# Row transposes two blocks ahead, a Newton inverse deviation, sorting by single operations and paired output projections in a convolution, attention and mixture-of-experts kernel

## The chip, the cores and the metric

The kernel runs on one core of a Trainium2 chip. The metric is the device time of one execution in microseconds, the median of several runs. The kernel before took 1325.14 us (three runs, 1323.45 to 1325.67). A core has five engines that run their own instruction lists in order and meet at semaphores: PE (TensorE, matrix products), ACT (ScalarE), DVE (VectorE), POOL (GpSimd) and SP (which only starts transfers here). PEld is PE's loading of the stationary operand.

## The reference

The input is two images of 256 channels and 56 x 56 pixels. Layer 0 is a grouped linear attention without softmax, folded with a normalisation, then a sum with its input and a ReLU. Layer 1 treats the 3136 pixels of each image as tokens of 256 numbers:

```
t = t + attn(ln(t))          # 4 heads of 64, causal softmax, then W_proj
x = ln(t)
probs = softmax(x @ gate_w + gate_b)          # 8 experts
top2_vals, top2_idx = top_k(probs, 2)
t = t + sum over the two experts e of  prob_e * (gelu(x @ W1[e] + b1[e]) @ W2[e] + b2[e])
```

`ln` subtracts the mean and divides by the square root of the variance plus 1e-5. All of it is computed in 32-bit floats.

## The kernel before

Layer 0 comes first, up to about 90 us. Then comes attention for image b=0 and for b=1, up to about 885 us, and then the experts, up to the end. From attention on, the order of every engine's instructions is the order in which the program writes them: nothing is moved by a scheduler.

**Attention** (`attend`). The queries of an image are cut in 7 blocks `i` of 448, and the heads in two pairs `hp`. One group is one (i, hp): it walks over tiles of 128 keys, one tile a step. In step n, in this order: `between` (other work, below), the tasks that have come due, `values` of the step three back (L689, the products of the exponentials with v), then `scores` of step n (L649 on PE, L657 exponentials on ACT, L659 mask on DVE, L671 or L667 the running sum of the exponentials, `acc`, on DVE). Where the step three back is the first of its group, `values` comes after `scores`. After the last `values` of a group the result is copied out of its one PSUM tile (L699 on ACT, then L700 on DVE adds the other half), and the next group's first `values` may only write that tile after L700. `values` then puts `sum_rows` on the list `later`, with the step at which it is due: it sums `acc` over the partitions on PE (L716, tile `sp`), and a chain of transfers through DRAM, `invert`, more transfers and `scale` (L748) brings the inverse back. The list is sorted when a task has run, and the head of the list is the only one looked at.

**Work beside attention.** `between` alternates: in one step it draws two pieces from `queue` (`pull(2)`), in the next it runs pieces of the projections to q, k and v (L535, L554, with transposes L514). A piece is what a generator does up to its next `yield True`. `tokens(b)` is the generator of the token work: `project_out` (L598, the output projection, tile by tile of 128 tokens, with DVE additions and statistics), then `dispatch`, which forms the gate, ranks the tokens by expert and scatters their rows to DRAM (L1217). For b=0 it runs beside b=1's attention; for b=1 it runs beside the experts, where each block draws two pieces, or three while rows are scattered.

In `dispatch`, `inverse_deviation` (L162) takes one ACT square root and one DVE reciprocal for all tokens. Then follow the softmax of the gate (L955 to L967, its exponential on ACT at L963), two rounds of choosing the best expert (L979 to L986), `both` (L991), the two PE products that rank the tokens (L1001, L1003), and some twenty small DVE operations that give every token its slot (to L1081). `small_piece` stands between groups of them: three yields for b=0, one for b=1.

**Experts** (`experts`). 105 blocks of 128 rows. Iteration n writes: the fetch of a group of three blocks (up to n+6), `load` (L1280 to L1289, DVE, up to n+2), `hidden(n)` (L1335 on PE, L1344 gelu on ACT), `inputs(n+1)` (transposes L1312 on PE, tile `tp`; the copy `xT`, L1316, on ACT), `weights` for the blocks ahead (L1323, DVE), `outputs(n-3)` (L1354 on PE, L1364 on DVE, then stores and scatters), and pieces. `hidden(n)` needs `xT` of block n and the weights copied for it. The tile pool of `xT` has three buffers, that of `tp` two.

Of the kernel before, what the change touches and what calls it, by code (L numbers as in the profile page):

```python
# [27 lines left out]
def conv_attn_moe_kernel(  # L28
# [410 lines left out]
    def layer1(nm, general):  # L439

        with ExitStack() as whole:
# [147 lines left out]
            def project_out(b, qT, done):  # L589

                for first, m, k in pairs():
                    while done() < (first + m - 1) * P + k:
                        yield False
                    for n in range(first, first + m):
                        o = n * P
                        ps = bank(f"pp_{b}_{n}")
                        for c in range(NH):
                            nc.tensor.matmul(  # L598
                                ps[:k, : C + E], qT[:, c, o : o + k], wpr[:, c, :],
                                start=(c == 0), stop=(c == NH - 1),  # L600
                            )
                        t = ts[b][:k, n, : C + E]
                        nc.vector.tensor_tensor(t, t, ps[:k, : C + E], ALU.add)
                        stats(b, n, 1, k, bg, f"o{nm}{b}")
                        if b == 0:
                            nc.sync.dma_start(out=rest_d[:k, n], in_=t[:, :C])
                        yield True

                    for _ in range(2 if b == 0 else 0):
                        yield True  # L610

            def attend(
# [63 lines left out]
                def values(n):  # L676
# [19 lines left out]
                    if last:  # L696

                        yh = qT[:, hp, i * W : (i + 1) * W]
                        nc.scalar.copy(yh, yp[:, 0, :W])  # L699
                        nc.vector.tensor_tensor(yh, yh, yp[:, 1, :W], ALU.add)  # L700
                        del yps[hp, i]
                        later.append((clock[0], sum_rows, hp, i, yh))

                def queue_of(hp, i):

# [229 lines left out]
            def dispatch(b):  # L935

                t = ts[b]
                tail = chunk(NCH - 1)
                inverse_deviation(b, 0, NCH)
                yield True  # L940

                def small_piece():

                    for _ in range(1 if b else 3):
                        yield True

                def small(name, last=E, dt=F32):
                    return g1.tile([P, NCH, last], dt, tag=name, name=f"{name}_{nm}{b}")

                def wide(ap):  # L950
                    return ap.to_broadcast([P, NCH, E])

                pr = small("lg")
                red = small("red", 1)
                nc.vector.tensor_tensor(  # L955
                    pr, t[:, :, C : C + E], wide(t[:, :, RSTD : RSTD + 1]), ALU.mult
                )
                nc.vector.tensor_tensor(
                    pr, pr, gb.unsqueeze(1).to_broadcast([P, NCH, E]), ALU.add
                )  # L960
                nc.vector.tensor_reduce(red, pr, AX.X, ALU.max)
                nc.vector.tensor_tensor(pr, pr, wide(red), ALU.subtract)
                nc.scalar.activation(pr, pr, AF.Exp)  # L963
                yield from small_piece()
                nc.vector.tensor_reduce(red, pr, AX.X, ALU.add)
                nc.vector.reciprocal(red, red)
                nc.vector.tensor_tensor(pr, pr, wide(red), ALU.mult)  # L967
                yield from small_piece()


# [5 lines left out]
                for k in range(2):  # L976
                    top = wts[b][:, :, k : k + 1]
                    one = small(f"one{k}")
                    nc.vector.tensor_reduce(top, src, AX.X, ALU.max)  # L979
                    nc.vector.tensor_tensor(at, src, wide(top), ALU.is_equal)  # L980
                    nc.vector.tensor_tensor(at, at, ids, ALU.mult)
                    yield from small_piece()
                    nc.vector.tensor_reduce(red, at, AX.X, ALU.max)
                    nc.vector.tensor_tensor(one, at, wide(red), ALU.is_equal)
                    if k == 0:
                        nc.vector.scalar_tensor_tensor(left, one, -2.0, pr, ALU.mult, ALU.add)  # L986
                        src = left
                    picks.append(one)
                    yield from small_piece()
# [7 lines left out]
                if b:  # L997
# [7 lines left out]
                nc.vector.tensor_tensor(  # L1005
                    ranks, rank[:, : NCH * E].rearrange("p (t e) -> p t e", e=E), both, ALU.subtract
                )
                tot = g1.tile([P, E, NCH], F32, tag="tot", name=f"tot_{nm}{b}")
                nc.vector.tensor_copy(tot, total[:, : NCH * E].rearrange("p (t e) -> p e t", e=E))
                yield from small_piece()  # L1010
                def few(name, dt=F32):
                    return g1.tile([P, E], dt, tag=name, name=f"{name}_{nm}{b}")
# [6 lines left out]
                else:  # L1019
# [11 lines left out]
                    ends.rearrange("p e t -> p (e t)"), ones_t,  # L1031
                    tot.rearrange("p e t -> p (e t)"), 0.0, ALU.mult, ALU.add,
                )

                first = few("first")
                nc.vector.tensor_tensor(first, ends[:, :, NCH - 1], cnt, ALU.subtract)
                nc.vector.tensor_tensor(ends, ends, tot, ALU.subtract)
                slot = g1.tile([P, NCH, E], F32, tag="both", name=f"slot_{nm}{b}")
                nc.vector.tensor_tensor(slot, ranks, ends.rearrange("p e t -> p t e"), ALU.add)
                yield from small_piece()  # L1040

                low = few("low")
# [22 lines left out]
                    return few.unsqueeze(1).to_broadcast([P, NCH, E])  # L1065

                nc.vector.tensor_tensor(part, slot, spread(lim), ALU.is_lt)
                nc.vector.tensor_tensor(part, part, spread(low), ALU.mult)
                yield from small_piece()
                nc.vector.tensor_tensor(slot, slot, spread(base), ALU.add)  # L1070
                nc.vector.tensor_tensor(slot, slot, part, ALU.add)
                yield from small_piece()
                for k in range(2):
                    nc.vector.tensor_tensor(at, slot, picks[k], ALU.mult)
                    nc.vector.tensor_reduce(red, at, AX.X, ALU.add)
                    flat = red.rearrange("p t o -> p (t o)")
                    nc.vector.tensor_scalar(
                        idxs[b][:, k, :], flat, -float(known[b][0] * P), None, ALU.add
                    )
                    if b and k == 0:  # L1080
                        nc.vector.tensor_scalar(t[:, :, SLOT], flat, 1.0, None, ALU.add)  # L1081
                    yield from small_piece()

                def one_hot(eb, w):

                    nc.vector.tensor_copy(eblks[b], eb[:, :w])
                    hot = g1.tile([E, w], F32, tag="hot", name=f"hot_{nm}{b}")
                    nc.vector.tensor_tensor(hot, eb[:E, :w], row.to_broadcast([E, w]), ALU.is_equal)
                    yield from small_piece()
                    for _ in range(1 if b else 3):  # L1090
                        yield True
                    bp = bank(f"bp_{b}", (P, KH, w))
                    for k in range(KH):
                        nc.tensor.matmul(bp[:, k, :], b1s[:, k, :], hot, start=True, stop=True)
                    nc.vector.tensor_copy(b1bs[b], bp)
                    ranked[b] = True
                    yield from small_piece()

                def first_blocks():
# [5 lines left out]
                        upto.unsqueeze(1).to_broadcast([P, MIXED, E]),  # L1105
                        ALU.is_ge,
                    )
                    eb = g1.tile([P, MIXED], F32, tag="eb", name=f"eb_{nm}{b}")
                    nc.vector.tensor_reduce(eb, past, AX.X, ALU.add)
                    yield from small_piece()  # L1110
                    step = g1.tile([P, MIXED], F32, tag="step", name=f"step_{nm}{b}")
                    nc.vector.tensor_scalar(step, number[:, :MIXED], nfull, -float(E), ALU.is_ge, ALU.mult)
                    nc.vector.tensor_tensor(eb, eb, step, ALU.add)
                    nc.vector.tensor_scalar(step, number[:, :MIXED], nfull, 0.0, ALU.subtract, ALU.max)
                    nc.vector.tensor_tensor(early, eb, step, ALU.add)
                    yield from one_hot(early, FULL0)
# [116 lines left out]
            def experts(w1s, w2s, b2s, ex, es, ps6, between, need, written):  # L1233
# [156 lines left out]
                for n in range(-1, NBLK + LATE):  # L1390
                    while len(fetched) * GB <= min(n + 6, NBLK - 1):
                        fetched.append(fetch(len(fetched)))
                    while len(groups) * GB <= min(n + 2, NBLK - 1):
                        groups.append(load(len(groups), *fetched[len(groups)]))
                    if n < 0:
                        ids.extend(experts_of(0))
                    if 0 <= n < NBLK:
                        act[n] = hidden(n, xin.pop(n), wb.pop(n))
                    if n + 1 < NBLK:
                        xin[n + 1] = inputs(n + 1, groups[(n + 1) // GB])  # L1400
                    for m in (n + 1, n + 2):
                        if m < NBLK and m not in wb:
                            wb[m] = weights(m)
# [416 lines left out]
```

## Time and profile before

| what | value |
|---|---|
| time | 1325.14 us, median of 3 |
| span of the profiled execution | 1323.5 us, granted PE clock 0.993 on the mean |
| PE idle in 60:130 us | 1.20 + 0.56 us |
| PE idle at 131, 199 and 517 us, before L689, until L700 | 1.49, 1.02 and 1.49 us |
| first expert block (L1335) | 886.58 us |
| last expert block ends | 1297.2 us |
| last row scatter of b=1 (L1217) | 1020.87 us |
| first fetch of rows of b=1 by blocks (L1256) | 1034.43 us |

The profile says for each group of instructions how long it was busy and what ended the idle time before it. A line of the timeline has: start in us, length in us, engine, source line, operation, written tile <- read tiles, the tile's size in the array, the shape, the number of instructions merged, and, in brackets, idle time before it and what ended it. The starts of matrix products are recorded; their ends are modelled, so the spacing of starts says more than the lengths.

### The profile page before, as it was taken

The page shows a single profiled execution, that of the slowest core. Times are in us where ns is not written, and L with a number is a line of the kernel's source. Part 1 is how long each engine was busy: PE and PEld are TensorE (multiplying, and loading weights), DVE is VectorE, ACT ScalarE, POOL GpSimd, SP SyncE. Part 2 cuts the span into 40 slices and gives each one's busy share as a digit, 9 for nine tenths or more (in the row PEclk, how much of TensorE's full clock was granted, in tenths as well). Part 3 has the DMA queues.
Part 4 walks back from the last instruction along what each step waited for, and adds up shares of the span by engine and source line. Part 5 has one row for each costly group of instructions (what it writes and reads, how often), then busy time and mean ns, then how long its engine had stood idle before and what let it go on. Part 6 is the DMA issues. An engine that isn't in the chain of part 4 may idle for free.

```text
span 1323.5 us, 28216 instructions
## 1 busy us (share of the span) xinstructions
PE 1281.4 (97%) x10647; PEld 811.4 (61%) x10647; DVE 791.9 (60%) x1657; ACT 613.2 (46%) x1247; POOL 311.8 (24%) x300
## 2 busy tenths in 40 slices
PE   8999999999999999989999999998999999999994
PEld 7875444444444444434444444447999999999994
DVE  1582555757777654565958788765754344555552
ACT  0145554555555555455554456554333333344441
POOL 1113110000000111110004444000176012765541
PEclk9999999999999999999999999999999999999997
DMA  9993000000000000100001112441254333666642
GB/s 298 384 327 131 16 24 25 24 16 24 9 17 13 21 1 8 41 9 9 16 17 56 53 54 87 176 139 40 81 169 156 93 112 100 187 208 198 187 153 71
DMA packets 111048, 123.96 MB, mean 94 GB/s; under 512 B 20095, under 2 KB 100620, under 8 KB 110904
## 3 DMA queue, kind: packets, MB, share of 16 engines
q1 hardware_dynamic: 96664, 92.89, 22.8%
q0 software_dynamic: 10416, 26.00, 5.9%
q10 hardware_dynamic: 3824, 3.18, 0.8%
q8 instruction: 88, 1.44, 0.5%
q14 instruction: 56, 0.46, 0.1%
HBM read 63.04 MB, written 60.81 MB: 94 GB/s over the span
## 4 chain that ended last, share of the span: by engine, by line
PE 92%; DVE 2%; ACT 2%; DMA 1%; issue 1%; POOL 1%; SPq 0%; DVEq 0%; ACTq 0%; POOLq 0%
PE yp_f L689 21%; PE sc_f L649 19%; PE ht_f L1335 14%; PE yp_f L1354 13%; PE qk_f L535 6%; PE pp_f L598 4%; PE v_f L554 4%; PE cp L321 3%; PE gram L252 3%; PE tp_f L1312 2%; ACT st_f L657 1%; PE sp_f L716 1%; PE yo_f L1477 1%; DVE acc_f L671 1%; PE xp_f L514 1%
## 5 line engine op out<-in xcount | busy, mean ns | idle before, releaser
L657 ACT ACTIVATE st_f<-sc_f 128x896 f32<-128x896 f32 (+5 forms) x400 | 333.8, 838 | 293.8 <-PE sc_f L649 265.4
L671 DVE TENSOR_TENSOR acc_f<-acc_f,st_f 128x896 f32<-128x896 f32 (+5 forms) x372 | 366.5, 985 | 170.0 <-ACT st_f L657 163.1
L689 PE MATMUL yp_f<-st_f,v_f 64*64 64x448 f32 (+6 forms) x3184 | 342.0, 505 | 7.7 <-DVE qT_f L700 6.5
L649 PE MATMUL sc_f<-qT_f,kT_f 64*64 64x448 f32 (+6 forms) x3184 | 342.3, 501 | 0.0
L1344 ACT ACTIVATE g_f<-ht_f,b1b 128x128 f32<-128x128 f32 x420 | 120.1, 369 | 223.5 <-PE ht_f L1335 223.4
L1335 PE MATMUL ht_f<-xT_f,w_f 128*128 128x128 f32 x1680 | 205.8, 276 | 5.8 <-ACT xT_f L1316 5.8
L649 PEld LDWEIGHTS sc_f<-qT_f,kT_f 64*64 64x64 f32 x3184 | 117.6, 133 | 151.7 <-issue 137.5
L689 PEld LDWEIGHTS yp_f<-st_f,v_f 64*64 64x64 f32 x3184 | 111.7, 133 | 159.3 <-issue 132.1
L1335 PEld LDWEIGHTS ht_f<-xT_f,w_f 128*128 128x128 f32 x1680 | 201.6, 192 | 12.5 <-ACT xT_f L1316 7.7
L497 POOL TENSOR_SCALAR xn_f<-t 128x256 f32<-128x256 f32 (+1 forms) x50 | 67.1, 1351 | 549.6 <-issue 333.6
L1217 POOL DMA_INDIRECT x_slots<-xr_f,idx x100 | 115.3, 1153 | 214.9 <-DVE xr_f L1209 136.4
L1323 DVE COPY w_f<-w1s_f 128x1024 f32 x105 | 73.8, 703 | 59.8 <-PE ht_f L1335 58.5
L1371 POOL DMA_INDIRECT y_tokens<-ys_f,to_f x63 | 64.4, 1022 | 148.7 <-DVE ys_f L1364 138.9
L535 PE MATMUL qk_f<-px_f,wat 128*128 128x512 f32 (+1 forms) x224 | 92.4, 558 | 1.2 <-ACT px_f L520 1.2
L1364 DVE TENSOR_TENSOR ys_f<-yp_f,kT_f 128x128 f32<-128x128 f32 x105 | 30.5, 291 | 102.8 <-PE yp_f L1354 102.7
L659 DVE TENSOR_TENSOR st_f<-st_f,keep 128x256 f32<-128x256 f32 (+1 forms) x112 | 44.1, 394 | 66.2 <-ACT st_f L657 65.8
L535 PEld LDWEIGHTS qk_f<-px_f,wat 128*128 128x128 f32 x224 | 38.6, 190 | 54.2 <-issue 44.8
L1354 PE MATMUL yp_f<-px_f,g_f 128*128 x210 | 62.7, 381 | 0.0
L1354 PE MATMUL yp_f<-v_f,g_f 128*128 x210 | 62.5, 379 | 0.0
L1354 PE MATMUL yp_f<-w2s_f,g_f 128*128 x210 | 62.5, 379 | 0.0
L1354 PE MATMUL yp_f<-kT_f,g_f 128*128 x210 | 62.5, 379 | 0.0
L1427 POOL DMA_INDIRECT y_f<-y_slots,idx x50 | 55.4, 1108 | 16.3 <-issue 14.0
(249 smaller groups left out, 1174.4 us busy)
## 6 DMA issues: line engine op xcount, KB each, us to landing
x_slots<-fill SPq DMA_DIRECT2D x1, 8127.0 KB
xb_f<-x_slots SPq DMA_DIRECT2D x63, 129.0 KB
x_slots<-fill SPq DMA_DIRECT2D x1, 7296.0 KB
y_slots<-ys_f SPq DMA_DIRECT2D x57, 128.0 KB
kept<-t SPq DMA_DIRECT2D x2, 3200.0 KB
x<-in_x_dram SPq DMA_DIRECT2D x14, 448.0 KB
xr<-in_x_rows_dram SPq DMA_DIRECT2D x12, 512.0 KB
out_dram<-ot_f SPq DMA_DIRECT2D x24, 256.0 KB
```

The lines of the kernel that those rows point to most:

```text
L497: nc.gpsimd.tensor_scalar(xn[:k, a], ts[b][:k, n + a, :C], ts[b][:k, n + a, MEAN : MEAN + 1], ts[b][:k, n + a, RSTD : RSTD + 1], ALU.subtr ...
L535: nc.tensor.matmul(ps[:, :w], wat[:, c, d0 : d0 + P], xT[:, c, :w], start=(c == 0), stop=(c == NH - 1),)
L649: nc.tensor.matmul(ps[h : h + HS, a, c0:W], kT[hp][rows, j * P + h : j * P + h + HS], qT[rows, hp, q0 + c0 : q0 + W], start=True, stop=True,)
L657: nc.scalar.activation(st[:k, :, c0:], ps[:k, :, c0:W], AF.Exp, scale=SCALE)
L671: nc.vector.tensor_tensor(acc[:k, :, c0:], acc[:k, :, c0:], st[:k, :, c0:], ALU.add)
L689: nc.tensor.matmul(yp[a * HS : (a + 1) * HS, h // HS, c0:W], v[hp][h : h + HS, j, a, :HS], st[h : h + HS, a, c0:], start=first, stop=bool( ...
L1217: s = nc.gpsimd.indirect_dma_start(out=xds[b], out_offset=bass.IndirectOffsetOnAxis(ap=idxs[b][:kk, k, n : n + 1], axis=0), in_=xr[:kk], i ...
L1323: nc.vector.tensor_copy(w, w1s[:, :, bass.ds(e, 1), :].rearrange("p c e h -> p c (e h)"))
L1335: nc.tensor.matmul(ht[:, k, :], w[:, c, k * P : (k + 1) * P], xT[:, c, :], start=(c == 0), stop=(c == NH - 1),)
L1344: nc.scalar.activation(g[:, k, :], ht[:, k, :], AF.Gelu, bias=b1bs[b][:, k, i : i + 1])
L1354: nc.tensor.matmul(yp[:, :C], g[:, k, :], w2s[k][:, bass.ds(e, 1), :].rearrange("p e d -> p (e d)"), start=(k == 0), stop=(k == KH - 1),)
L1371: s = nc.gpsimd.indirect_dma_start(out=y_tokens, out_offset=bass.IndirectOffsetOnAxis(ap=to[:, n % GB : n % GB + 1], axis=0), in_=ys, in_o ...
```

## The change

It has five parts. (1) `inputs` is written two blocks ahead of `hidden` instead of one, and `load` one block earlier. (2) The inverse deviation of `dispatch` is computed on DVE, by a first guess from the bits of the number and four Newton steps, so that ACT needs no square root there. (3) For b=0 the operations of `dispatch` are single pieces, by a new `op`, which yields for b=0 only, and `small_piece` yields for b=1 only. (4) A pair of token tiles of `project_out` is one piece. (5) `sum_rows` is due one step later. The purpose is to take long runs of DVE work, and waits of ACT for DVE, out of PE's way.

```diff
@@ project_out
                         stats(b, n, 1, k, bg, f"o{nm}{b}")
                         if b == 0:
                             nc.sync.dma_start(out=rest_d[:k, n], in_=t[:, :C])
-                        yield True
-
-                    for _ in range(2 if b == 0 else 0):
+
+                    for _ in range(4 if b == 0 else 2):
                         yield True
@@ values
-                        later.append((clock[0], sum_rows, hp, i, yh))
+                        later.append((clock[0] + 1, sum_rows, hp, i, yh))
@@ dispatch
-                inverse_deviation(b, 0, NCH)
-                yield True
                 def small_piece():
-                    for _ in range(1 if b else 3):
+                    if b:
+                        yield True
+
+                def op():
+                    if b == 0:
                         yield True
...
+                var = t[:, :, RSTD]
+                x, y, z = (
+                    small(k, 1).rearrange("p t o -> p (t o)") for k in ("newton_x", "newton_y", "red")
+                )
+                nc.vector.tensor_scalar(x, var, 1e-5, None, ALU.add)
+                nc.vector.tensor_scalar(
+                    y.bitcast(I32), x.bitcast(I32), 1, None, ALU.arith_shift_right
+                )
+                nc.vector.tensor_scalar(
+                    y.bitcast(I32), y.bitcast(I32), -1.0, float(0x5F3759DF), ALU.mult, ALU.add
+                )
+                yield from small_piece()
+                for i in range(4):
+                    to = var if i == 3 else y
+                    nc.vector.tensor_tensor(z, y, y, ALU.mult)
+                    nc.vector.tensor_tensor(z, z, x, ALU.mult)
+                    nc.vector.tensor_scalar(z, z, -0.5, 1.5, ALU.mult, ALU.add)
+                    nc.vector.tensor_tensor(to, y, z, ALU.mult)
+                    yield from op()
+                    yield from small_piece()
...
                 nc.vector.tensor_tensor(pr, pr, wide(red), ALU.subtract)
+                yield from op()
+                yield from small_piece()
                 nc.scalar.activation(pr, pr, AF.Exp)
                 yield from small_piece()
+                yield from op()
                 nc.vector.tensor_reduce(red, pr, AX.X, ALU.add)
+                yield from op()
...
                     nc.vector.tensor_tensor(one, at, wide(red), ALU.is_equal)
+                    yield from op()
...
@@ one_hot
-                    for _ in range(1 if b else 3):
+                    for _ in range(1 if b else 4):
                         yield True
@@ experts
-                    while len(groups) * GB <= min(n + 2, NBLK - 1):
+                    while len(groups) * GB <= min(n + 3, NBLK - 1):
                         groups.append(load(len(groups), *fetched[len(groups)]))
...
-                    if n + 1 < NBLK:
-                        xin[n + 1] = inputs(n + 1, groups[(n + 1) // GB])
+                    for m in (n + 1, n + 2):
+                        if m < NBLK and m > n + 1 - (n < 0):
+                            xin[m] = inputs(m, groups[m // GB])
```

The remaining hunks add `yield from op()` after each further wide operation of `dispatch` and of its block table. There is none between `both` (L991) and the product that ranks the tokens (L1001); the old `small_piece` stands there.

## The prediction

> **What bounds the kernel.** I read the busy time first, then the chain of waits by engine, then PE's own waits.
>
> ```profile
> PE 1281.4 (97%) x10647; PEld 811.4 (61%) x10647; DVE 791.9 (60%) x1657; ACT 613.2 (46%) x1247; POOL 311.8 (24%) x300
> ...
> PE 92%; DVE 2%; ACT 2%; DMA 1%; issue 1%; POOL 1%; SPq 0%; DVEq 0%; ACTq 0%; POOLq 0%
> ```
>
> PE is the bound, so only PE's gaps count. They sum to 42 us, of which 6.3 are at the start and 18 in the tail after the last block, which no part of the change touches. What can be won stands in PE's waits:
>
> ```profile
> PE yp_f L689 <- DVE qT_f L700: 6.5, 5, 1.7
> ...
> PE ht_f L1335 <- ACT xT_f L1316: 5.8, 6, 1.4
> PE sp_f L716 <- ACT v_f L563: 2.5, 1, 2.5
> ```
>
> The columns are us in total, times, longest. With 0.6 for a mask (L659) at 602 us, that is 15 us at most. Between 925 and 1300 us no PE wait is listed, and a block takes 3.73 us with nothing beside it: the experts' steady part has nothing to give.
>
> The 2.5 us gap, from PE's timeline, and the clock granted after it, from the windows (PE busy, PEld, DVE, ACT, POOL, PEclk, DMA share, GB/s):
>
> ```profile
> 572.70 0.59 PE L716 MATMUL sp_f<-acc_f,ones 128*32 128x224 f32 x8 [2.52 <-ACT v_f L563]
> ...
> 571.14 0.37 ACT L963 ACTIVATE lg_f<-lg_f 128x200 f32<-128x200 f32 x1 [3.13 <-DVE lg_f L962]
> ...
> 574.00:576.00 2.00, 2.00 (x20) 0.91 (x16) 0.00 (x0) 0.49 (x1) 0.00 (x0) 0.50 0.01 2
> 576.00:578.00 2.00, 2.00 (x17) 0.57 (x10) 1.69 (x4) 0.21 (x1) 0.00 (x0) 0.66 0.04 2
> ```
>
> ACT stood 3.13 us behind the gate's exponential, which waited for four DVE operations; the copy of v that frees PE's bank was queued behind it. Then the clock fell: 2 x 0.50 + 2 x 0.34 = 1.7 us more. This gap cost 4.2 us.
>
> Last, the end of a group of attention, one of many alike:
>
> ```profile
> 809.01 0.93 PE L689 MATMUL yp_f<-st_f,v_f 64*64 64x448 f32 x8
> 809.76 0.93 PE L649 MATMUL sc_f<-qT_f,kT_f 64*64 64x448 f32 x8
> 810.62 0.59 PE L716 MATMUL sp_f<-acc_f,ones 128*32 128x224 f32 x8
> 811.14 0.98 PE L649 MATMUL sc_f<-qT_f,kT_f 64*64 64x448 f32 x8
> 811.94 1.73 PE L689 MATMUL yp_f<-st_f,v_f 64*64 64x448 f32 x16
> ...
> 810.26 1.09 DVE L671 TENSOR_TENSOR acc_f<-acc_f,st_f 128x896 f32<-128x896 f32 x1 [0.39 <-ACT st_f L657]
> 811.27 0.61 DVE L700 TENSOR_TENSOR qT_f<-qT_f,yp_f 128x448 f32<-128x448 f32 x1
> ```
>
> L700 ends at 811.88, and the new group's first values start 0.06 us later, at 811.94. So far `sp` fills the time on PE: no gap is seen, but there is no slack either.
>
> [...] The trace has the half clock (0.50), but already after 2.5 us idle; the gap of 1.72 us at 590 was followed by none. [...] The trace shows loads of 1.28 us, and the square root 0.02 us behind one (561.93, then 563.23)[...]; I count 1.28. [...]
>
> **The change, part by part.**
>
> *Paired projections* (part 4): before, `pull(2)` took two tiles in one draw already (L598 appears as x8); b=0 has 4 yields a pair before and after. Only the last single tile gains one. Zero: hidden in a queue of pieces with slack.
>
> *Gate and sorting for b=0* (parts 2, 3). Removed: the 2.52 us gap, since the exponential now comes a draw after its input, and with it 1.7 of clock. At 590 to 592, PE waited 1.72 for L700 behind three sorting operations (3 x 0.37) and L748 (0.62); most goes, but two operations a draw remain: 1.2. The 0.6 at 602 goes. The two table loads and the square root (2.9 us on ACT, 561.9 to 565.3) lay beside PE work: nothing. Sum -6.0.
> Added: Newton is 3 + 4 x 4 = 19 operations of 128x25. No 25-wide tensor-tensor is in the trace; the nearest rows are 0.18 (L1077, a scalar operation) and 0.32 (L167, reciprocal)[...]. I take 0.2: 11 in the first draw, 2.2 us, 8 in the next. Behind them on DVE queue the additions to `acc`, masks and L700; PE sees that only if a group ends there: 0 to 1.5, I take 0.5.
> And a new wait: for b=0 `both` and the ranking product (L1001) are now in one piece. On PE's list L1001 comes directly behind the last scores. Those scores must go through ACT (0.24 until it starts, 0.95), the sum (1.0), `one`, `both` and a memset (0.40 + 0.40 + 0.10), and 0.06 back: 3.1 us for a full tile, 2.1 for the narrowest (exponential 0.28, mask and sum 0.29 each). All of PE is queued behind. I take 2.6, and half of another clock dip, 0.8. Sum +3.4.
>
> *`sum_rows` a step later* (part 5). `sp` then comes after the first values instead of before. L700 stays where it is: its chain (scores, two exponentials, sum, L700) does not contain `sp`. So PE idles until 811.94 and pays for `sp` after it: 0.52, plus 0.11 for the change of tile size (0.86 against 0.75 between starts), 0.6 in all. Of 28 group ends, 11 are of this kind: nine as shown (253, 317, 379, 409, 449, 706, 782, 812, 849 us) and the two that already wait (131, 517). At 643 the removed 0.8 and the added 0.6 cancel. Where q, k, v or projection products stand between (12 ends), at the last end, or where `sp` already comes after (158, 199, 592), it costs nothing; at 199, L748 falls behind L700, -0.5. Sum 11 x 0.6 - 0.5 = +6.1.
>
> *Rows two blocks ahead* (part 1), with b=1's gate. In the transition the six waits are 0.16, three of 1.28, 0.41 and 1.36.
>
> ```profile
> 902.21 0.63 DVE L748 TENSOR_TENSOR qT_f<-qT_f,rb_f 128x448 f32<-128x448 f32 x1 [5.45 <-DMA rb_f<-inverses]
> 902.75 1.29 DVE L1323 COPY w_f<-w1s_f 128x1024 f32 x2
> ...
> 903.58 2.02 PE L1335 MATMUL ht_f<-xT_f,w_f 128*128 128x128 f32 x16
> ```
>
> The first four are not won: block 4 waits for its weights, queued on DVE behind L748, which waits for the last group's transfers, begun by `sp` at 885.83. Blocks 0 to 3 only finish earlier and wait. The second transpose and its copy even delay `sp`: +0.4; and the waits merge into one of some 4 us, so a clock dip is possible: +0.8 in all. The 0.41 and 1.36 came from table loads and the gate's exponential on ACT; with `xT` a block further ahead they go: -1.8. `load` a block earlier leaves 11 us from issue to use instead of 15; the landing median in x_slots is 3.1: hidden. `dispatch` for b=1 has 22 pieces instead of 17, and the last projection one more: three blocks, 11 us. The last scatter moves from 1021 to about 1032, just before the fetch at 1034 (landing: 3 us): hidden, with little to spare.
>
> Sum: -6.0 + 0.5 + 3.4 + 6.1 + 0.8 - 1.8 = +3.0. 1325.1 + 3.0 = 1328.1.
>
> **Rivals.** *A, faster*: moving `sp` is free, because L700 comes earlier or other work fills in. Then 1328.1 - 6.6 = 1321.5. For it: nowhere in the trace of before is a gap of this kind shown in the nine places; against it: the 0.06 us and 199, where `sp` comes after and PE waits. *B, no change*: half of the moves cost, or the ranking wait is 2.1 without a dip: about 1325. *C, worse*: clock dips after the ranking wait, at 131 and 517 (gaps then near 2.1 us) and in the transition, 1.7 each, or scatters that hold up the fetch: 1328.1 + 5 = 1333. Against it: only one gap so far brought a dip.
>
> **Chances.** Forecast 0.40, A 0.26, B 0.22, C 0.12. Taken alone, A lies below 1322.5 (0.2%), B within, the other two above 1327.8: faster 0.26, same 0.22, slower 0.52. The range goes from A with the low ranking wait (1321.5 - 1.5) to C: 1320 to 1333.
>
> **What would show it.** Right: no wait of `sp` for v near 570; a PE wait at L1001 of 2 to 3 us; at the ends named, waits of 0.5 to 0.6 at L689 for L700, whose total rises from 6.5 to about 11; no wait for `xT` after 905; the blocks start some 4 us later than 886.58 (-6.0 + 0.5 + 3.4 + 6.1), and block 4 still 17 us after the first. Wrong: no new waits at L689, or a first block before 886, or PE waits between 1030 and 1060.

## The result and the profile after

The changed kernel takes 1336.57 us (median of 4 runs, 1335.61 to 1339.59) against 1324.91 us before (4 runs, 1323.45 to 1325.67): a ratio of 1.0093, 95% interval 1.0075 to 1.0111. It is slower by 11.7 us (0.9%), where +3.0 was forecast.

Below line 690 the change shifts the line numbers by one (L689 is now L688, L700 L699, L716 L715, L748 L747, L659 L658), the ranking product L1001 is L1040, and in the experts L1335 is L1390, L1312 is L1367 and L1323 is L1378.

First the busy times of the page, and the chain of waits by engine:

```profile
PE 1283.8 (96%) x10647; PEld 813.3 (61%) x10647; DVE 796.6 (60%) x1693; ACT 608.2 (46%) x1241; POOL 313.9 (24%) x300
...
PE 88%; DVE 5%; ACT 2%; DMA 2%; issue 1%; POOL 1%; SPq 0%; ACTq 0%; DVEq 0%; POOLq 0%
```

The number of PE instructions is the same, and PE is 2.4 us busier. The span grew by 11 us, so most of the loss is idle time of PE. DVE's share of the chain rose from 2% to 5%. PE's waits (us in total, times, longest) name the lines:

```profile
PE yp_f L688 <- DVE qT_f L699: 12.8, 14, 2.6
...
PE yp_f L688 <- DVE st_f L658: 3.2, 3, 1.8
PE rank_f L1040 <- DVE both_f L1032: 3.1, 1, 3.1
PE ht_f L1390 <- DVE w_f L1378: 2.7, 1, 2.7
...
PE tp_f L1367 <- DMA xb_f<-x_slots: 1.0, 1, 1.0
```

The wait of `sp` for v and those for `xT` are gone, as the change meant. The wait for L700 went from 6.5 us in 5 places to 12.8 in 14, masks from 0.6 to 3.2, and the ranking product is new. PE's timeline shows three of these places, with the former gap at 570 first:

```profile
576.15 0.58 PE L715 MATMUL sp_f<-acc_f,ones 128*32 128x224 f32 x8
...
595.04 1.25 PE L688 MATMUL yp_f<-st_f,v_f 64*64 64x448 f32 x8 [2.63 <-DVE qT_f L699]
...
628.73 0.58 PE L1040 MATMUL rank_f<-both_f,keep 128*128 128x200 f32 x2 [3.06 <-DVE both_f L1032]
...
650.98 0.45 PE L688 MATMUL yp_f<-st_f,v_f 64*64 64x128 f32 x8 [1.80 <-DVE st_f L658]
```

`sp` at 576 waits for nothing. The two gaps at 595 and 628 are each followed by a dip of the granted clock. The windows show the first one (PE, PEld, DVE, ACT, POOL busy, then PEclk, DMA share, GB/s):

```profile
594.00:596.00 2.00, 0.96 (x8) 0.21 (x8) 2.00 (x4) 0.00 (x0) 0.00 (x0) 0.91 0.00 0
596.00:598.00 2.00, 2.00 (x20) 0.58 (x20) 1.68 (x3) 0.34 (x1) 0.00 (x0) 0.50 0.00 0
598.00:600.00 2.00, 2.00 (x24) 0.72 (x20) 0.00 (x0) 0.09 (x1) 0.00 (x0) 0.74 0.04 10
```

2 x (0.09 + 0.50 + 0.26) = 1.7 us are lost; at 628 to 634 it is 1.7 again (0.94, 0.50, 0.71). Before there was one dip, at 574 to 577 us (the tail, from about 1308 us before and 1319 us after, is at a granted clock of 0.50 in both). DVE's timeline tells why L699 was late at 595:

```profile
593.82 0.62 DVE L747 TENSOR_TENSOR qT_f<-qT_f,rb_f 128x448 f32<-128x448 f32 x1 [1.23 <-DMA rb_f<-inverses]
594.37 0.62 DVE L699 TENSOR_TENSOR qT_f<-qT_f,yp_f 128x448 f32<-128x448 f32 x1
```

The scaling of the group before, L747, stood 1.23 us for its transfer, and L699, which PE needs, was queued behind it. L699's own inputs were ready by 591.6 us, when ACT's copy (L698) had ended. The end of a group of the kind that the prediction showed now looks like this, at two places:

```profile
319.40 0.98 PE L688 MATMUL yp_f<-st_f,v_f 64*64 64x448 f32 x8 [0.33 <-DVE qT_f L699]
320.31 0.58 PE L715 MATMUL sp_f<-acc_f,ones 128*32 128x224 f32 x8
...
825.44 0.98 PE L688 MATMUL yp_f<-st_f,v_f 64*64 64x448 f32 x8 [0.80 <-DVE qT_f L699]
826.35 0.58 PE L715 MATMUL sp_f<-acc_f,ones 128*32 128x224 f32 x8
```

`sp` follows the first values, and PE waits ahead of them. The idle time named is shorter than the cost. Setting the start of L699 in every group against that of L700 in the kernel before, seven ends up to 526 us added 0.64 to 0.68 us each. Last, the start of the experts:

```profile
900.92 2.05 PE L1390 MATMUL ht_f<-xT_f,w_f 128*128 128x128 f32 x16
...
911.09 2.02 PE L1390 MATMUL ht_f<-xT_f,w_f 128*128 128x128 f32 x16 [2.73 <-DVE w_f L1378]
...
917.44 2.02 PE L1390 MATMUL ht_f<-xT_f,w_f 128*128 128x128 f32 x16
```

The blocks start 14.3 us later than before (886.58), and block 4 comes 16.5 us after the first (17.0 before). So the whole loss arises in attention; the profiled span as a whole is 11.3 us longer (1334.8 against 1323.5), so some 3 us are given back after that.

One new wait there was not in the forecast: PE stood 0.97 us at 905.95 for a row transfer (`xb`), since the transposes now ask for their rows a block sooner.

### The profile page after: what moved, and what is told of

It reads as the page before. It is cut to its first block, busy times and chain, and to the rows that moved or that the text cites. A ratio compares the mean times of both kernels' runs of the same rounds, so it can differ in the third digit from the quotient of the medians.

```text
span 1334.8 us, 28229 instructions
## 1 busy us (share of the span) xinstructions
PE 1283.8 (96%) x10647; PEld 813.3 (61%) x10647; DVE 796.6 (60%) x1693; ACT 608.2 (46%) x1241; POOL 313.9 (24%) x300
## 4 chain that ended last, share of the span: by engine, by line
PE 88%; DVE 5%; ACT 2%; DMA 2%; issue 1%; POOL 1%; SPq 0%; ACTq 0%; DVEq 0%; POOLq 0%
PE yp_f L688 19%; PE sc_f L648 17%; PE ht_f L1390 14%; PE yp_f L1409 13%; PE qk_f L535 7%; PE v_f L554 4%; PE pp_f L598 3%; PE cp L321 3%; PE gram L252 3%; DVE acc_f L670 2%; ACT st_f L656 2%; PE tp_f L1367 2%; PE sp_f L715 1%; PE yo_f L1533 1%; PE xp_f L514 1%
## 5 line engine op out<-in xcount | busy, mean ns | idle before, releaser
L688 PE MATMUL yp_f<-st_f,v_f 64*64 64x448 f32 (+6 forms) x3184 | 347.0, 507 | 16.5 <-DVE qT_f L699 12.8
L688 PEld LDWEIGHTS yp_f<-st_f,v_f 64*64 64x64 f32 x3184 | 110.1, 133 | 168.9 <-issue 130.4
L1390 PE MATMUL ht_f<-xT_f,w_f 128*128 128x128 f32 x1680 | 205.5, 276 | 2.7 <-DVE w_f L1378 2.7
L1390 PEld LDWEIGHTS ht_f<-xT_f,w_f 128*128 128x128 f32 x1680 | 201.8, 192 | 8.2 <-issue 3.7
L1378 DVE COPY w_f<-w1s_f 128x1024 f32 x105 | 73.8, 704 | 60.3 <-PE ht_f L1390 60.0
L535 PE MATMUL qk_f<-px_f,wat 128*128 128x512 f32 (+1 forms) x224 | 92.4, 558 | 1.2 <-ACT px_f L520 1.2
L658 DVE TENSOR_TENSOR st_f<-st_f,keep 128x256 f32<-128x256 f32 (+1 forms) x112 | 44.3, 395 | 68.0 <-ACT st_f L656 67.4
L535 PEld LDWEIGHTS qk_f<-px_f,wat 128*128 128x128 f32 x224 | 38.7, 190 | 54.2 <-issue 43.8
```

The source lines that it names most:

```text
L535: nc.tensor.matmul(ps[:, :w], wat[:, c, d0 : d0 + P], xT[:, c, :w], start=(c == 0), stop=(c == NH - 1),)
L688: nc.tensor.matmul(yp[a * HS : (a + 1) * HS, h // HS, c0:W], v[hp][h : h + HS, j, a, :HS], st[h : h + HS, a, c0:], start=first, stop=bool( ...
L1378: nc.vector.tensor_copy(w, w1s[:, :, bass.ds(e, 1), :].rearrange("p c e h -> p c (e h)"))
L1390: nc.tensor.matmul(ht[:, k, :], w[:, c, k * P : (k + 1) * P], xT[:, c, :], start=(c == 0), stop=(c == NH - 1),)
```

## The experiments

All times are medians of 4 to 21 executions, against runs of the kernel before on the same chip (about 1325 us, but for the last group). The experiments ran on several chips.

**Each part alone.** Rows two blocks ahead (part 1), put into the kernel before:

```diff
-                    if n + 1 < NBLK:
-                        xin[n + 1] = inputs(n + 1, groups[(n + 1) // GB])
+                    for m in (n + 1, n + 2):
+                        if m < NBLK and m > n + 1 - (n < 0):
+                            xin[m] = inputs(m, groups[m // GB])
```

> The kernel before, with the expert rows transposed two blocks ahead (and their load one block earlier) and nothing else. Theory (the first four waits for xT only hide the transfers of the last group, the two later ones are won): 1 to 1.5 us faster, about 1323.7, with the start of block 4 at most 0.5 us later than before. Rival (each wait for xT was a loss): 5.8 us faster, 1319. Second rival (the earlier load makes DVE wait for rows): slower than before.

1323.12 us, ratio 0.9988 (0.9981 to 0.9994): a gain of 1.6. The six waits for `xT` (5.8 us) are gone; PE waits 2.8 us for weights and 1.8 for a row transfer in their place.

The sums a step later (part 5), put into the kernel before:

```diff
-                        later.append((clock[0], sum_rows, hp, i, yh))
+                        later.append((clock[0] + 1, sum_rows, hp, i, yh))
```

> The kernel before, with the row sums of attention due one step later and nothing else. Theory (the row sums filled the time in which PE waits for L700): at 11 to 12 group ends PE now waits and pays 0.66 us each, as the starts of the changed kernel show; 7 to 8 us slower, about 1332.5. Rival (the later row sums are free, and all of the loss is in the gate and sorting of b=0): 1325, within 1 us.

1334.2 us, ratio 1.0069 (1.0055 to 1.0083): 9.5 us slower. The rival is out, and the loss is more than expected. The seven ends up to 526 us cost 0.63 to 0.68 us each here too; the profile also has a gap of 2.25 us at 648 with a clock dip behind it.

The changed kernel with that one line put back:

> The changed kernel, with the row sums due as before. Theory: 7 to 8 us faster than the changed kernel, about 1329; the waits of L688 for the copy of the result outside the sorting stage go. Rival (row sums free): 1336.5.

1321.32 us, ratio 0.9972 (0.9961 to 0.9982). Parts 1 to 4 together gain 3.6 us, 1.6 of them from part 1. The one line costs 15.3 us in their company, where 6.1 was forecast and 9.5 measured alone. All that follows asks why.

**Larger draws.** The changed kernel with the old groups of operations for b=0 and the old three yields after each (`op` empty):

> The changed kernel, with the operations of the gate and the sorting grouped in pieces with three yields as before for b=0 (and one for b=1); Newton steps, later row sums, rows two blocks ahead and paired projections stay. Theory (the pieces without yields cost PE the wait at the ranking product, 3.1 us, its clock dip, 1.7, and about 5 us of waits behind runs of narrow operations): 8 to 10 us faster than the changed kernel, about 1327.5. Rival (the Newton steps as such load DVE, whatever the pieces): at most 3 us faster, 1334 or more.

1344.21 us, ratio 1.0135. The test says nothing on its question: three yields at each of some 23 places are more than the 41 single ones, the token work of b=0 came too late, and PE paid at the end, as its waits show:

```profile
PE pp_f L598 <- DVE qT_f L747: 18.0, 1, 18.0
```

The granted clock was 0.50 from 896 to 916 us there, so some 2.6 us more were lost in the slow products after the wait.

With two yields instead of three, and the sums due as before:

> The changed kernel with the sums due as before, and for b=0 the sorting in the old groups of two to four operations with two yields after each group (about 46 yields) instead of single operations with one yield each (about 41), so that the sorting ends at about the same time. Theory: a group holds up masks and L699 by 0.4 to 0.8 us more at the two or three ends it meets, and the exponential of the gate again has its input in the same draw's group: 1321.3 + 1.5 = 1323. Rival: single operations bring nothing by themselves: 1321.3; or the sorting ends too late and the projections of b=1 wait for it again: over 1330, with a wait of several us on L598.

1319.93 us, ratio 0.9962 (0.9949 to 0.9976), within the interval of 1321.32's. The groups also put two yields ahead of the ranking product, so the closer match is the kernel with single operations and those yields, below (1320.13). The theory fell: with the sums as before, sorting by single operations brings nothing that can be measured over groups of them with two yields.

**Mending single gaps of the changed kernel.** Two yields ahead of the ranking product:

```diff
-                if b:
+                for _ in range(1 if b else 2):
                     yield True
```

> The changed kernel, with two yields instead of none between `both` and the ranking product of b=0 (one for b=1 as before), so that a step of attention is put on PE's list between them. Theory: the 3.06 us wait of the ranking product for `both` and the clock dip that follows it (1.7) go, and nothing else moves: 1336.6 - 4.8 = 1331.8. Rival: attention stands still for the same chain of scores, exponential and sum anyway, so the wait only moves to the next group's end: 1336, with waits of 2 to 3 us on L688 near 628 in place of it.

1333.64 us: 2.9 of the 4.8 came. The ranking wait is gone, but PE's timeline has a longer gap near 653, with a clock dip at 654 to 660 (the profiled execution was the slowest of the five, so how often that dip comes is not shown):

```profile
653.88 0.98 PE L688 MATMUL yp_f<-st_f,v_f 64*64 64x448 f32 x8 [3.06 <-DVE qT_f L699]
```

`scale` two steps later:

```diff
-                    later.append((clock[0] + 4, lambda hp, i, yh: scale(hp, i, yh, rb), hp, i, yh))
+                    later.append((clock[0] + 6, lambda hp, i, yh: scale(hp, i, yh, rb), hp, i, yh))
```

> The changed kernel, with `scale` (the product with the inverses, L747, which waits on DVE for a DMA) due six steps after the sums instead of four. Theory: the 2.63 us wait of the first values for L699 near 595 comes from L747 standing ahead of L699 in DVE's queue for 1.23 us for its transfer; with L747 later that wait falls to about 1.2[...]: 1336.6 - 1.4 - 1.7 = 1333.5. Rival: the wait comes from the narrow sorting operations on DVE, and moving L747 changes nothing: 1336.6; or worse, L747 falls on another group's end and costs as much there.

1333.63 us, as expected, but only half by the way expected. The gap at 595 fell from 2.63 to 1.58 and its dip, the 1.7 in the expected time, went. Near 653 a gap of 3.40 with a dip came, in place of 1.80 and 1.81 without one. The edit does more than the expectation says: `hand_on` is due two steps after `scale`, so it comes two steps later as well, and the sorting moved. DVE's timeline has a group's end (L699) and the first operation of `dispatch`:

```profile
566.69 0.61 DVE L699 TENSOR_TENSOR qT_f<-qT_f,yp_f 128x448 f32<-128x448 f32 x1
...
583.32 0.17 DVE L963 TENSOR_SCALAR newton_x_f<-t 128x25 f32<-128x25 f32 x1
```

These are 16.6 us apart; in the changed kernel they are 11.6 apart (below). So this run does not single out L747.

Five more yields among the narrow operations (DVE operations of 8 elements a partition):

> The changed kernel, with five more single-operation yields of b=0 among the narrow sorting operations that run as one string on DVE (ten and more in a row before the mask of 650.5). Theory: the waits of 650.98 (1.80), 656.25 (1.81) and 671.51 (1.14) for L658 and L699 come from that string; shorter strings take some 2 to 3 us of these 4.75: 1334. The other two gaps (595, 628) stay, at 2.6 and 3.1. Rival: the group ends there have no slack at all with the sums a step later, so that any DVE work delays them: no change, 1336.6, or somewhat more because the sorting lasts longer.

1337.19 us: no change. The waits did fall near where expected (1.80 near 650 is 0.97, the 1.14 at 671 is gone), but a third clock dip came at 656 to 660, and other gaps grew (2.63 is 2.88). So the shorter strings won nothing that lasted; that they cost nothing is not shown.

**The ranking yields with the sums as before**, and then with the narrow yields as well:

> The changed kernel with the sums due as before and the two yields ahead of the ranking product of b=0, nothing else. Theory: the 2.31 us wait of the ranking product goes, no clock dip was behind it: 1321.3 - 2.3 = 1319.0; the narrow yields then account for the rest down to 1318.1. Rival: the wait comes back at the next group's end: 1321.

> The changed kernel with three things: sums due as before (as in the run of that alone, 1321.3), the two yields ahead of the ranking product, and the five yields among the narrow operations. Theory: from 1321.3 the ranking wait (2.3, no dip) goes and about half of the mask waits (1.8): 1321.3 - 2.3 - 0.9 = 1318, below both kernels. Rival: the waits that are left follow from how much DVE work there is in the stage and only change places: 1321.

1320.13 us (0.9970, 0.9959 to 0.9981) and 1318.11 us (0.9949, 0.9936 to 0.9962). The first is not clear of 1321.32 (0.9961 to 0.9982). In it the 2.31 us ranking wait is gone, but a mask wait grows from 0.87 us (sums as before alone) to 1.59:

```profile
637.09 0.45 PE L688 MATMUL yp_f<-st_f,v_f 64*64 64x128 f32 x8 [1.59 <-DVE st_f L658]
```

In the second that wait is 0.77 and no clock dip is left between 520 and 920 us. It is the best version found: 6.8 us below the kernel before, 18.5 below the changed one.

**Where the later sums cost.** For b=0 alone (`clock[0] + (1 if b == 0 else 0)`), and for b=1 alone:

> The changed kernel with the sums a step later only for the groups of b=0, whose attention lies beside no sorting (up to about 500 us); for b=1 they are due as before. Theory: each moved `sp` costs 0.67 us there and nothing else follows, since the delay only shifts all later work alike: 1321.3 (sums as before everywhere) + 7 x 0.67 = 1326. Rival: the delay itself upsets the sorting that comes after it, so that most of the 15.3 us is back: 1330 or more.

> The changed kernel with the sums a step later only for the groups of b=1, beside whose attention b=0 is sorted. Theory: the excess over the price of the moves arises here, by the order in which L747, the narrow operations and `both` stand ahead of L699 on DVE: 1321.3 + 15.3 - 4.7 = 1332, with waits of 2 to 3 us near 590, 625 and 650 and clock dips behind them. Rival: only 6 moved ends at 0.67 count here, 1325.5.

1333.0 us (1.0066, 1.0052 to 1.0079) and 1326.98 us (1.0021, 1.0013 to 1.0029). The theory fell. The sums of b=0, beside which nothing is sorted, cost 11.7 us, those of b=1 5.7 (17.4 in all, over 15.3: `sp` of the end at 517 comes after the first values in both). With b=0's sums late, the ranking wait is 3.06 us and the mask wait 1.60, as in the changed kernel; with b=1's they are 2.30 and at most 0.86. So something that b=0's groups start moves the sorting. DVE's timeline shows it, first with the sums as before, then in the changed kernel (a group's end L699, and the first operation of `dispatch`):

```profile
563.21 0.62 DVE L699 TENSOR_TENSOR qT_f<-qT_f,yp_f 128x448 f32<-128x448 f32 x1
...
569.19 0.17 DVE L963 TENSOR_SCALAR newton_x_f<-t 128x25 f32<-128x25 f32 x1
```

```profile
568.64 0.58 DVE L699 TENSOR_TENSOR qT_f<-qT_f,yp_f 128x448 f32<-128x448 f32 x1
...
580.19 0.18 DVE L963 TENSOR_SCALAR newton_x_f<-t 128x25 f32<-128x25 f32 x1
```

The sorting starts 6.0 us after the group in one, 11.6 in the other. A later `sum_rows` makes `invert`, `scale` and `hand_on` later by a step. `hand_on` is what lets the output projections of b=0 begin, and a draw comes only at every second step. The projection that comes first after b=0's last group starts at 535.20 and 545.18, 8.5 and 13.1 us after the group end before it. The whole sorting moves along against the attention of b=1.

**Taking the two effects of the one line apart.** `hand_on` is due two steps after `scale`. With later sums and one step, the sorting stands where it did; with sums as before and three steps, only the sorting moves:

```diff
-                    later.append((clock[0] + 2, hand_on, hp, i, yh))
+                    later.append((clock[0] + 1, hand_on, hp, i, yh))
```

> The changed kernel, sums a step later as in the change, but a group is handed on one step after its scaling instead of two, so that the projections and the sorting of b=0 stand against attention where they do with the sums as before. Theory (the shift of the sorting is the cause of the excess): 1321.3 + 11 x 0.67 = 1328.7, the first projection 8.5 us after the group end near 527 and not 13. Rival (the later L747 and `sp` themselves disturb DVE in the sorting): 1336, no gain.

> The changed kernel with the sums due as before, but a group is handed on three steps after its scaling instead of two, so that only the projections and the sorting move, as in the changed kernel. No matrix product of the sums moves. Theory: 1321.3 + (11.7 - 7 x 0.67) = 1328.3, with waits near 595, 627 and 650 like those of the changed kernel. Rival (the shift of the sorting costs nothing): 1321.3.

1359.04 and 1352.68 us: these fell on a chip on which the kernel before takes 1368 us. They were run again on a second chip of that kind (kernel before 1367.88 us), with both ends beside them:

> The changed kernel with the sums due as before, as the base for the two hand-on kernels on the same chip. On a chip where the kernel before takes about 1325 us: 1321.3 as in its first run, 15 us below the changed kernel.

> Sums a step later, groups handed on a step sooner, so that the sorting stands where it does with the sums as before. Theory (the shift of the sorting is the excess over the moves): 7.4 us (11 x 0.67) above the sums-as-before kernel. Rival (the shift costs nothing): as slow as the changed kernel, 15 above.

> Sums as before, groups handed on a step later, so that only projections and sorting move. Theory: 15.3 - 7.4 = 8 us above the sums-as-before kernel (7 by the run with the sums of b=0 alone), with waits of 2.0, 3.1, 1.8, 1.1 and 1.1 us near 587, 619, 641, 647 and 661. Rival: no difference from the sums-as-before kernel.

> The changed kernel itself, as the other end on the same chip: 15 us above the kernel with the sums as before, and its 15 the sum of the two hand-on kernels' excesses, 7.4 and 8.

| kernel, on this chip | sums | sorting | us | above the first |
|---|---|---|---|---|
| sums back | as before | in place | 1348.54 (1346.28 to 1349.83) | |
| hand-on sooner | a step later | in place | 1355.62 (1352.97 to 1359.38) | +7.1 |
| hand-on later | as before | moved | 1352.65 (1350.58 to 1354.91) | +4.1 |
| the changed kernel | a step later | moved | 1365.46 (1361.36 to 1370.67) | +16.9 |

On this chip the whole change is no loss: 1365.46 against 1367.88 (0.9987, 0.9973 to 1.0001), and with the sums back it is 19.3 us faster (0.9853). In the experts PE has waits there that the profile puts down to no engine (6.9 us in 17 places before L1390 with the sums back, none in that kernel's first run) and more clock dips; that does not make up the whole difference between the chips, and why they differ is open.

In "sorting moved" the sorting starts 11.55 us after its group in both kernels, in "in place" 5.97 and 5.86. For hand-on later:

```profile
561.92 0.58 DVE L699 TENSOR_TENSOR qT_f<-qT_f,yp_f 128x448 f32<-128x448 f32 x1
...
573.47 0.17 DVE L963 TENSOR_SCALAR newton_x_f<-t 128x25 f32<-128x25 f32 x1
```

The moves of `sp` by themselves cost 7.1, where 11 x 0.67 = 7.4 was expected. The moved sorting by itself costs 4.1, half of what was expected. PE's timeline of that kernel (hand-on later) has it, without any moved `sp`:

```profile
587.76 0.98 PE L688 MATMUL yp_f<-st_f,v_f 64*64 64x448 f32 x8 [2.08 <-DVE qT_f L699]
...
619.87 0.58 PE L1040 MATMUL rank_f<-both_f,keep 128*128 128x200 f32 x2 [3.06 <-DVE both_f L1032]
...
640.47 0.45 PE L688 MATMUL yp_f<-st_f,v_f 64*64 64x128 f32 x8 [1.79 <-DVE st_f L658]
645.73 1.74 PE L688 MATMUL yp_f<-st_f,v_f 64*64 64x448 f32 x16 [1.13 <-DVE qT_f L699]
...
660.24 0.66 PE L688 MATMUL yp_f<-st_f,v_f 64*64 64x256 f32 x8 [1.06 <-DVE st_f L658]
```

These are the changed kernel's gaps, a little shorter. With 0.53 for a copy of v they sum to 9.65 us; with the sums back on the same chip the gaps over 0.5 us of this stage are 1.17, 2.31, 0.58, 0.86 and 0.81, 5.73 in all. The difference of 3.9 agrees with the 4.1 measured, as far as runs that spread over 4 us can show it.

The two effects add up to 11.2, and 5.7 of the 16.9 are left. That remainder is not firm: the hand-on-sooner kernel's first runs, with 1359.04, would leave 2.3. The four profiles say more. From PE's first L535 that waits for `px` (96.56, 96.43, 96.06 and 95.55 us, in the order of the table) to the first transpose of the experts (886.80, 895.12, 890.24 and 907.02 us), hand-on sooner takes 8.4 us more than the first kernel, hand-on later 3.9 and the changed one 21.2. In that stretch the changed kernel has five clock dips, each of the others one. Less 4 x 1.7 us it takes 14.4 more, against 12.4 for the two effects. So most of what arose when they met is clock dips, in these executions; the changed kernel's was the slowest of its 16 (1370.67 us).

## Why the prediction was wrong

The direction was right and the mechanism at the group ends was right; the sum was short by 8.7 us, and nearly all of that lies in one term, **`sum_rows` a step later, +6.1**, which measured 15.3. Two sentences of it failed.

*"Where q, k, v or projection products stand between (12 ends), at the last end, or where `sp` already comes after (158, 199, 592), it costs nothing"* and *"At 643 the removed 0.8 and the added 0.6 cancel."* The term followed `sum_rows` only to PE's list. It did not follow the tasks that hang on it (`invert`, `scale`, `hand_on`) to the draw that starts the sorting, although the described code has that chain. At 592 (now 595) PE lost 2.63 us and 1.7 of clock, near 643 (now 651 and 656) 1.80 and 1.81. From the starts of L699 the cost of the line, changed kernel against sums back, can be laid out by stage:

| stage (time in the kernel before) | forecast, us | cost, us | of this |
|---|---|---|---|
| up to 545 | 7 x 0.6 - 0.5 = 3.7 | 5.5 | seven moved ends, 7 x 0.67 = 4.7; 0.3 was there before attention |
| 545 to 781, beside the sorting | 0.6 | 9.2 | gaps of PE over 0.5 us 10.97 instead of 5.74: 5.2; two clock dips: 3.4 |
| 781 to 886 | 3 x 0.6 = 1.8 | 2.3 | three moved ends: 1.0, 0.67, 0.61 |

They add up to 17.0; the two profiled spans differ by 16.1, so 0.9 comes back in the experts. The ends outside the sorting were priced nearly right: 0.67 each instead of 0.6, and the 0.5 hoped for at 199 did not come (the offset to the kernel before stayed within 0.13 us there). The stage in the middle was taken as free of it, but for one end.

The other steps, in the order of the prediction:

- *Paired projections, 0*: not run alone. Parts 2 to 4 together (sums back, less part 1 alone) gave -1.8 us, and the forecast for them was -6.0 + 0.5 + 3.4 = -2.1. Right as a sum, by some luck: in the profile with the sums back the ranking wait is 2.31 without a dip instead of 3.4, the gap near 590 only fell from 1.72 to 1.17 where 0.5 was to be left, and waits of 0.58, 0.87, 0.36 and 0.41 for v and masks came that had no term.
- *The gap of 2.52 at 570 and its clock dip go*: right; `sp` at 576.15 waits for nothing.
- *Newton, 0.2 each*, the author's estimate: 0.18 to 0.19 as a rule (580.19 is one of them), 11 in a string in the first draw. No group end fell on them.
- *The ranking wait: "3.1 us for a full tile, 2.1 for the narrowest"*: right at the upper end. The changed kernel has 3.06; the unmoved sorting has 2.31. A dip follows the 3.06 in both profiles of the changed kernel. The 2.6 + 0.8 taken was 1.4 too low for the changed kernel, and which of the two ends holds is again set by where the sorting stands.
- *Rows two blocks ahead, -1.0*: -1.6, the sign and the place right. The merged wait was 2.73 us, and 0.97 for a row transfer, which was taken as hidden: 3.7 instead of some 4. A clock dip followed the 2.84 us wait of part 1 alone (898 to 902 us), none the 2.73 of the changed kernel (granted clock 1.00 in every window from 908 to 918 us).
- *The last scatter*, hidden: right. It moved to 1043.25 us and the fetch to 1046.12; no PE wait is listed between 1030 and 1060 us.
- *Blocks start some 4 us later*: 14.3.

Of the rivals, C named clock dips as the way to something worse. The one after the ranking wait came. Of those at 131, at 517 and in the transition, the changed kernel's profile in the result has none, that on the slower chip has the one at 131. The dip after the gap at 595 was in no rival, and C's 1333 falls short too. A is refuted by the kernel with only the sums moved (+9.5), and so is B as far as it had half of the moves free.

What stays open: how much more the two effects cost together than apart, and why the clock dips then come more often. In the changed kernel's two profiles there are two and four clock dips beside the sorting, against none and one with the sums back. L747 also stands ahead of L699 at 595 there. No run takes that wait away without moving the sorting, so what it costs by itself is not shown.

## What to carry to other kernels

When a task in a hand-written order is delayed, follow everything it hands on, down to the draw or queue that it releases; a delay of one step of 1.5 us moved the whole sorting by 5.6 us against attention. What a piece of side work costs depends on which step of the main loop it falls beside, so effects of parts need not add: the later sums cost 9.5 alone and 15.3 in company. Run the whole change with one part undone, not only each part alone. And a gap taken away in a queue that is this full tends to come back at the next place: 2.9 of 4.8 us were kept in one case, 1.2 of 2.3 in another (within the spread of the runs), and nothing with the yields among the narrow operations.

## What was not expected of the hardware

Whether the clock falls after a gap is not decided by the gap's length alone. The same kernel with the sums back, the same ranking wait, on two chips; windows after it:

```profile
616.00:618.00 2.00, 2.00 (x16) 0.83 (x8) 0.00 (x0) 0.92 (x1) 0.00 (x0) 1.00 0.00 0
```

```profile
616.00:618.00 2.00, 2.00 (x13) 0.38 (x5) 0.00 (x0) 0.00 (x0) 0.00 (x0) 0.50 0.00 0
```

Both follow a wait of 2.31 us, at 614.4. A wait of 3.06 us had no dip in the run with b=0's sums late, and one of 1.50 us had a dip in the changed kernel with the ranking yields (132 to 138 us: 0.80, 0.50, 0.84). In the hand-on-later kernel a dip follows a wait of only 1.06 us, at 660.24, and none its waits of 2.08 and 3.06:

```profile
662.00:664.00 2.00, 2.00 (x14) 1.10 (x17) 1.86 (x4) 0.69 (x1) 0.00 (x0) 0.67 0.00 0
664.00:666.00 2.00, 2.00 (x13) 0.50 (x6) 1.00 (x3) 0.10 (x1) 0.70 (x1) 0.50 0.00 0
```

Each of these dips is a loss of 1.7 us by its 2 us windows. Windows of 0.5 us on the changed kernel's first dip (595.5 to 599.5 us: 0.62, six of 0.50, 0.96) put its length at 3.4 us, and the same windows on its second (629.5 to 633.5 us: 0.76, six of 0.50, 0.83) give 3.4 us too. In the experts one lasted twice as long: after a wait of 2.89 us at 908.88 in the changed kernel with the ranking yields (908 to 916 us: 0.51, 0.50, 0.50, 0.78), a loss of 3.4 us.

A gap of 1 to 3 us cost its length and nothing, 1.7 or 3.4 us more in these runs. What decides which is not shown.
